# Layer 0 of a four-layer graph network: the bias of r and the candidate written into PSUM by ScalarE instead of two matmuls

## The chip, the core and the metric

One core of a Trainium2 chip runs the whole kernel in one launch. The metric is the device time of the launch in microseconds (us). A profile is taken of one further execution; its span goes from the first to the last instruction of the program, and the execution's own time is about 2 us longer.

## The reference, cut to what matters

Four layers follow each other, each with a residual and a layer norm. Layer 0 is a recurrence over the 256 nodes of each of 64 graphs, with 256 features. It is the only layer that the change touches:

```python
d = jnp.sum(adj, axis=-1)
dinv = jnp.where(d != 0, 1.0 / jnp.where(d != 0, d, 1.0), 0.0)
norm_adjT = jnp.swapaxes(adj, 1, 2) * dinv[:, :, None]

def step(h, i):
    x = jnp.take(h_e, i, axis=1)
    row = jnp.take(norm_adjT, i, axis=1)
    x_par = jnp.einsum('bj,bjd->bd', row, h)
    iou = x @ W_ioux.T + b_ioux + x_par @ W_iouh.T + b_iouh
    r, z = jnp.split(iou, 2, axis=1)
    r, z = (jax.nn.sigmoid(r), jax.nn.sigmoid(z))
    hc = jnp.tanh(x @ W_coux.T + b_coux + x_par * r @ W_couh.T + b_couh)
    h_new = z * x_par + (1.0 - z) * hc
    h = jax.lax.dynamic_update_slice(h, h_new[:, None, :], (0, i, 0))
    return (h, None)
```

Step i needs the state that step i - 1 has just written (through `x_par`), so the 256 steps can't run side by side. Layers 1 to 3 are a graph convolution, a masked attention and an eight-head attention, each done for one graph after another.

## The kernel before, in words

The layout of a state is 128 partitions by 128 columns: partition `o * 64 + b` holds graph b and the half o of the 256 features. The products need the features on partitions, so `xp` (the reference's `x_par`) and `rx` (r times `xp`) are transposed by TensorE and copied to SBUF by ScalarE (`flip`, L594 to L599, giving `xpT` and `rT`).

Layer 0 is one loop over the step n (L706 to L843). The order in which the instructions are written is the order on every engine's queue; no scheduler moves them. T = 32 steps share tables, U = 8 steps share a tile of sums `ACC`, and p = n % 8 decides which side work a step carries. Each step does this:

- The transpose of `xp` on TensorE, and its copy `xpT` on ScalarE. VectorE adds the state h of the step before (L630), ScalarE copies it to `hs` (L632).
- `h_part` multiplies `xpT` with the weights of r (four matmuls, L746) and of z (four, L768). Between and after them stand pieces of side work that TensorE does for later steps: `late` (p from 0 to 3) and `early` or the x side (p from 4 to 7).
- VectorE pushes h into the sums of the next steps (`push`, L614), GpSimd into those further away (`push_far`, L641 to L650), and GpSimd makes `ready` for the next step (L751 to L755).
- ScalarE takes the sigmoid of r (L776), the sigmoid of -z (`zc`, L780) and of z (L781). VectorE multiplies r with `xp` (`rx`, L778).
- `flip` transposes `rx` and copies it to `rT` (L782).
- For the next step, a new PSUM tile `rc` (two of them in turn, a bank each; it holds r in its first 128 columns, the candidate in its last) gets its bias (`bias_part`, L788) and the first half of its x products (L789).
- `h_part` adds the candidate's products with `rT` (L790).
- ScalarE copies up to two PSUM banks of side work to SBUF (`next_of(copies, n)`, L791 and L811). TensorE goes on with the second half of the x products (L798), and the bias and x products of the next z (L799 to L802).
- ScalarE takes the tanh of the candidate (L805). VectorE makes `v` from `ready` (L796), then `zcc` = (1 - z) times the candidate (L807), then the next `xp` (L810).

`bias_part` is one bf16 matmul for each half o, with a contraction of three: the bias is split into three bf16 parts, and the stationary operand is three rows of ones. It opens the accumulation in the bank; all the other products add:

```python
nc.tensor.matmul(
    G[o * B:(o + 1) * B], ones3, bias3[:, o, gates], start=True, stop=False,
    skip_group_check=True,
)
```

`G` is the PSUM tile, `gates` picks r and candidate (columns 0 and 1, so 256 columns) or z (column 2, so 128). PSUM is full: three banks for side work, two for `rc`, one each for z, for the transposes and for `keep`, which holds states and intermediates.

Of the kernel before, what the change touches and what calls it, by code (L numbers as in the profile page):

```python
# [9 lines left out]
F32 = mybir.dt.float32  # L10
# [9 lines left out]
P = 128  # L20
# [50 lines left out]
def _recurrence(tc, ident, Hd, x, adj, W_ioux, b_ioux, W_iouh, b_iouh, W_coux, b_coux, W_couh, b_couh):  # L71
# [18 lines left out]
    nc = tc.nc  # L90
# [12 lines left out]
    with ExitStack() as ctx:  # L103
        const = ctx.enter_context(tc.tile_pool(name="r_const", bufs=1))
# [2 lines left out]
        WhT = const.tile([P, 2, 2, 3, P], F32, name="WhT")  # L107
        bias3 = const.tile([3, 2, 3, P], BF16, name="bias3")
        ones3 = const.tile([3, B], BF16, name="ones3")
        tri = const.tile([P, P], F32, name="tri")  # L110
        window = [const.tile([P, T], F32, name=f"window{w}") for w in range(2)]
        dinv = const.tile([P, N], F32, name="dinv")
# [10 lines left out]
        with tc.tile_pool(name="r_setup", bufs=1) as tmp, tc.tile_pool(  # L123
            name="r_setup_ps", bufs=2, space=bass.MemoryType.PSUM
# [59 lines left out]
        with tc.tile_pool(name="r_first", bufs=2) as tmp, tc.tile_pool(  # L184
            name="r_first_ps", bufs=4, space=bass.MemoryType.PSUM
# [27 lines left out]
        ps = ctx.enter_context(tc.tile_pool(name="r_ps", bufs=1, space=bass.MemoryType.PSUM))  # L213
# [356 lines left out]
        def bias_part(G, gates):  # L570
            for o in range(2):
# [5 lines that stand above are left out]
        def x_part(G, n, kc, gates):  # L577
            a, u = divmod(n, U)
            h, i = divmod(u, U // 2)
            for o in range(2):  # L580
                nc.tensor.matmul(  # L581
                    G[o * B:(o + 1) * B], xqT[a, i // 2][:, i % 2, kc, h * B:(h + 1) * B],
                    WxT[:, kc, o, gates], start=False, stop=False, skip_group_check=True,
                )
# [9 lines left out]
        def flip(src, tag, n):  # L594
            pt = ps.tile([P, P], F32, tag="flip", name=f"{tag}_ps_{n}")
            nc.tensor.transpose(pt, src, ident)  # L596
            t = new(tag, n, 1)
            nc.scalar.copy(t, pt)  # L598
            return t  # L599

        def new(tag, n, bufs=2):
            return work.tile([P, P], F32, tag=tag, name=f"{tag}_{n}", bufs=bufs)
# [7 lines left out]
        def push(count):  # L610
            for _ in range(min(count, len(pushes))):
                m, j = pushes.pop(0)
                acc, s = cell(j, m)
                nc.vector.scalar_tensor_tensor(  # L614
                    acc[:, 0, :], keep[:, j % 2, :], s, acc[:, 0, :], ALU.mult, ALU.add
                )
# [56 lines left out]
        rc = ps.tile([P, 2, P], F32, tag="rc", name="rc_0", bufs=2)  # L673
        z = ps.tile([P, P], F32, tag="z", name="z_ps_0")
        for G, gates in ((rc, slice(0, 2)), (z, 2)):
            bias_part(G, gates)
            for kc in range(2):
                x_part(G, 0, kc, gates)

# [26 lines left out]
        for now in range(N):  # L706
            n = now
            k, i = divmod(n, T)
            p = n % U
            last = n + 1 == N  # L710
# [37 lines left out]
                push(1)  # L748
            if not last:
                kk, ii = divmod(n + 1, T)  # L750
                ready = new("ready", n)  # L751
                nc.gpsimd.tensor_mul(  # L752
                    ready, sums[(n + 1) // U][:, (n + 1) % U, :],
                    dinv[:, n + 1:n + 2].to_broadcast([P, P]),
                )  # L755
# [23 lines left out]
            zc = new("zc", n, 1)  # L779
            nc.scalar.activation(zc, z, AF.Sigmoid, scale=-1.0)  # L780
            nc.scalar.activation(z, z, AF.Sigmoid)  # L781
            rT = flip(rx, "rT", n)  # L782
            push(1)
            zx = keep[:, 2, :]
            nc.vector.tensor_mul(zx, z, xp)
            if not last:
                rc = ps.tile([P, 2, P], F32, tag="rc", name=f"rc_{n + 1}", bufs=2)
                bias_part(rc, slice(0, 2))  # L788
                x_part(rc, n + 1, 0, slice(0, 2))  # L789
            h_part(c, 1, rT)  # L790
            for _ in range(2 if p == 3 else 1):  # L791
# [513 lines left out]
@with_exitstack  # L1305
def kernel(ctx: ExitStack, tc: tile.TileContext, ins, out):
    nc = tc.nc
    x, adj = ins["x"], ins["adj"]
    B, N, D = x.shape
    main = ctx.enter_context(tc.tile_pool(name="main", bufs=1))  # L1310
    dram = ctx.enter_context(tc.tile_pool(name="dram", bufs=1, space=bass.MemoryType.DRAM))
    ident = main.tile([P, P], F32, name="ident")
    make_identity(nc, ident)
    Hd = dram.tile([N, B, D], F32, name="Hd")
    _recurrence(
        tc, ident, Hd, x, adj,
        *(ins["L0_gnn_" + n] for n in (
            "W_ioux", "b_ioux", "W_iouh", "b_iouh", "W_coux", "b_coux", "W_couh", "b_couh"
        )),
    )  # L1320
    l2, l3 = (
        {w + n: ins[f"{l}_gnn_{w}{n}"] for w in "Wb" for n in "vkqo"} for l in ("L2", "L3")
    )
    Yd = dram.tile([B, P, 2, D], F32, name="Yd")
    found = _layers(tc, ident, Hd, Yd, x, adj, ins["L1_gnn_W"], ins["L1_gnn_b"], l2, l3, out)
    with tc.If(found > 0):
        _layer_3(tc, ident, Yd, adj, l3, out)
# [36 lines left out]
```

## Time and profile before

| what | value |
|---|---|
| median of 3 runs | 3620.76 us (3611.67 to 3627.42) |
| profiled execution, its own time | 3625.61 us |
| its span | 3623.6 us |
| layer 0's steps in it | about 150 to 1590 us |
| granted TensorE clock | 0.975 |
| busy over the span | PE 92%, PEld 66%, DVE 66%, ACT 51%, POOL 41% |
| bias matmuls of rc (L572) | 512, median 292 ns |
| bias matmuls of z (L572) | 512, median 238 ns |

PE is TensorE's matmuls, PEld its weight loads, DVE VectorE, ACT ScalarE, POOL GpSimd, SP the queue that issues most DMAs. Matmuls are pipelined, so the length of one bar is longer than the time that it keeps the next one waiting; the starts of neighbours tell more. A row of the timeline has the start and the length in us, engine, line, operation, the tile written and the tiles read, the shapes, a count, and in brackets the idle time of the engine before it and what ended it. In the table of waits, a row names who waited, for whom, the total in us, the number of times and the longest. A row of the groups ends with the busy time in us, the mean length in ns, and the idle time before it.

### The profile page before, as it was taken

Reading aid. Unit: us, or ns where it says so; the run is one execution under the profiler, and the core shown is the slowest. Engines: PE = TensorE matmul, PEld = TensorE weight load, DVE = VectorE, ACT = ScalarE, POOL = GpSimd, SP = SyncE. Lnnn points to the kernel's source line nnn. Section 1 sums busy time; section 2 is a strip of 40 time slices with the busy share of each in tenths; the row PEclk is TensorE's granted clock in tenths of the full one; section 3 lists DMA queues with packets and bytes.
Section 4 is the critical chain, followed back from the end, with each engine's and each line's share of the span. In section 5 each row is a group of like instructions: output and inputs, shape, how many; then the busy total and the mean of one; then the engine's idle time right before and its main releaser. Section 6 shows DMA issues by size and latency. Waiting matters only on the chain.

```text
span 3623.6 us, 81902 instructions
## 1 busy us (share of the span) xinstructions
PE 3338.4 (92%) x30882; PEld 2384.0 (66%) x30882; DVE 2374.3 (66%) x7052; ACT 1836.0 (51%) x4771; POOL 1487.7 (41%) x1669
## 2 busy tenths in 40 slices
PE   5599999999989998858999999999999999999998
PEld 4455555555555555536777777777777777777776
DVE  2366766766667777734777677666677777776765
ACT  0144444444434444424666666666666666666664
POOL 2266666766556777722222222222222222222221
PEclk9799999999999999978999999999999999999999
DMA  8746566687876563240111111111111111111100
GB/s 279 219 129 142 155 170 154 147 189 201 192 186 167 150 165 106 67 107 29 45 45 45 45 45 45 45 45 45 45 45 45 45 45 44 43 45 45 45 27 22
DMA packets 389637, 348.51 MB, mean 96 GB/s; under 512 B 107244, under 2 KB 355192, under 8 KB 384120
## 3 DMA queue, kind: packets, MB, share of 16 engines
q1 hardware_dynamic: 367280, 323.84, 33.6%
q10 hardware_dynamic: 21960, 19.41, 1.6%
q8 instruction: 245, 4.01, 0.5%
q14 instruction: 152, 1.25, 0.1%
HBM read 224.01 MB, written 99.61 MB: 89 GB/s over the span
## 4 chain that ended last, share of the span: by engine, by line
PE 74%; POOL 6%; DMA 6%; DVE 6%; issue 4%; ACT 3%; SPq 2%; ACTq 0%; DVEq 0%; POOLq 0%
PE mm L940 13%; PE o L1143 7%; PE rc L581 4%; PE rc L589 4%; PE s L1123 4%; PE mm_2f L940 3%; PE mm_3v L940 3%; PE mm_3f L940 3%; PE mm_t L940 3%; PE mm_g L940 3%; PE mm_2s L940 3%; PE mm_2v L940 3%; PE mm_2w L940 3%; PE late L505 3%; PE tr_x L930 3%
## 5 line engine op out<-in xcount | busy, mean ns | idle before, releaser
L614 DVE SCALAR_TENSOR_TENSOR ACC<-keep,S,ACC 128x128 f32<-128x128 f32 x1712 | 504.5, 345 | 191.4 <-ACT hs L632 175.8
L909 POOL TENSOR_TENSOR rstd<-rstd,mhalf 128x2 f32<-128x2 f32 x256 | 173.1, 694 | 627.8 <-DVE rstd L908 626.1
L650 POOL TENSOR_TENSOR ACC<-ACC,far 128x384 f32<-128x384 f32 (+1 forms) x313 | 371.9, 1188 | 24.5
L1130 DVE TENSOR_TENSOR p<-s,neg 128x512 f32<-128x512 f32 x512 | 317.7, 683 | 68.6 <-PE s L1123 68.6
L581 PE MATMUL rc<-WxT,xqT 128*64 128x256 f32 x2048 | 329.8, 401 | 1.8 <-issue 1.8
L917 ACT ACTIVATE y<-y,shift,rstd 128x256 f32<-128x256 f32 x512 | 273.5, 598 | 95.3 <-DVE shift L915 91.0
L1035 POOL TENSOR_TENSOR y<-y,g 128x512 f32<-128x512 f32 x64 | 81.2, 1269 | 565.4 <-issue 556.4
L646 POOL TENSOR_TENSOR far<-hs,S 128x384 f32<-128x384 f32 (+1 forms) x313 | 304.8, 974 | 4.7
L1131 ACT ACTIVATE p<-p 128x512 f32<-128x512 f32 x512 | 295.0, 627 | 2.6 <-DVE p L1130 1.6
L752 POOL TENSOR_TENSOR ready<-ACC,dinv 128x128 f32<-128x128 f32 x255 | 102.3, 401 | 419.0 <-DVE ACC L614 397.9
L905 DVE BATCH_NORM_STATS2 st<-y 128x6 f32<-128x256 f32 x512 | 209.1, 408 | 93.8 <-POOL y L1035 89.0
L1158 DVE TENSOR_TENSOR y<-y,mm_3f 128x512 f32<-128x512 f32 x64 | 44.0, 688 | 281.3 <-PE mm_3f L940 281.3
L1149 DVE RECIPROCAL rT<-o 128x256 f32<-128x256 f32 x128 | 224.1, 1751 | 0.3 <-PE o L1143 0.3
L1046 ACT ACTIVATE qk<-mm,b_cols 128x256 f32<-128x256 f32 x256 | 107.4, 470 | 202.6 <-PE mm L940 202.6
L1021 ACT COPY xT<-tr_x 128x512 f32<-128x512 f32 x192 | 112.4, 587 | 182.7 <-PE tr_x L930 182.7
L589 PE MATMUL rc<-WhT,xpT 128*64 128x128 f32 x2048 | 170.2, 287 | 28.1 <-ACT xpT L598 28.0
L598 ACT COPY xpT<-xpT_ps 128x128 f32<-128x128 f32 x256 | 68.3, 267 | 245.5 <-PE xpT_ps L596 245.5
L589 PEld LDWEIGHTS rc<-WhT,xpT 128*64 128x64 f32 x2048 | 107.7, 137 | 117.8 <-ACT xpT L598 84.1
L807 DVE TENSOR_TENSOR zcc<-zc,rc 128x128 f32<-128x128 f32 x256 | 72.8, 284 | 155.1 <-ACT rc L805 155.1
L581 PE MATMUL z_ps<-WxT,xqT 128*64 128x128 f32 x2048 | 171.0, 289 | 0.0
L940 PE MATMUL mm<-xT,W2q 128*128 128x256 f32 x512 | 129.4, 396 | 44.7 <-ACT xT L1021 44.7
L1098 ACT ACTIVATE qk<-mm,b_cols 128x256 f32<-128x256 f32 x256 | 107.5, 471 | 118.2 <-PE mm L940 118.2
(165 smaller groups left out, 7980.2 us busy)
## 6 DMA issues: line engine op xcount, KB each, us to landing
xX<-in_x_dram ACTq DMA_DIRECT2D x16, 1024.0 KB
Us<-xu SPq DMA_DIRECT2D x64, 256.0 KB
rows<-in_adj_dram SPq DMA_DIRECT2D x64, 256.0 KB
ACC<-Us SPq DMA_DIRECT2D x32, 512.0 KB
xq<-in_x_dram SPq DMA_DIRECT2D x64, 256.0 KB
Hw<-hs SPq DMA_DIRECT2D x512, 32.0 KB
Es<-eu SPq DMA_DIRECT2D x64, 256.0 KB
early_sb<-Es SPq DMA_DIRECT2D x32, 512.0 KB
```

What stands on the lines that cost most here:

```text
L581: nc.tensor.matmul(G[o * B:(o + 1) * B], xqT[a, i // 2][:, i % 2, kc, h * B:(h + 1) * B], WxT[:, kc, o, gates], start=False, stop=False, s ...
L589: nc.tensor.matmul(G[o * B:(o + 1) * B], hT[:, kc * B:(kc + 1) * B], WhT[:, kc, o, g], start=False, stop=(kc == 1), skip_group_check=True,)
L614: nc.vector.scalar_tensor_tensor(acc[:, 0, :], keep[:, j % 2, :], s, acc[:, 0, :], ALU.mult, ALU.add)
L646: nc.gpsimd.tensor_mul(tmp[:, 0:count, :], hs.unsqueeze(1).to_broadcast(shape), s.unsqueeze(2).to_broadcast(shape),)
L650: nc.gpsimd.tensor_add(acc, acc, tmp[:, 0:count, :])
L905: nc.vector.bn_stats(st, y[:, c, :])
L917: nc.scalar.activation(y[:, c, :], y[:, c, :], AF.Identity, bias=shift[:, c:c + 1], scale=rstd[:, c:c + 1],)
L940: nc.tensor.matmul(pm[:, c, :], lhsT[:, k, c * P:(c + 1) * P], rhs[:, k, :], start=(k == 0), stop=(k == 1),)
L1130: nc.vector.tensor_add(p, s_ps[i], self.neg3)
L1131: nc.scalar.activation(p, p, AF.Exp, scale=ISQ)
L1143: nc.tensor.matmul(o_ps[i * HD:(i + 1) * HD, part, :], ones if part else self.v3_sb[:, k, h * HD:(h + 1) * HD], self.ps_of[hc][i][:, k, :] ...
L1149: nc.vector.reciprocal(rT, o_ps[:, 1, :])
```

## The change

A new SBUF tile `bias_rc` (128 x 256 fp32) keeps the bias of r and candidate as it stands in PSUM: it is copied once, from the first `rc`, right after `bias_part` has filled it. From step 1 on, the next `rc` gets its bias by a ScalarE copy of `bias_rc`, which stands on ScalarE's queue after the sigmoid of z and ahead of the copy `rT`. The x and h products then add to what ScalarE wrote; none of them opens the bank. In step 0 the next `rc` still gets its bias by matmuls, so both banks of `rc` have been opened once. The bias of z stays a matmul. To make room, `ready` has one buffer instead of two.

```diff
         ones3 = const.tile([3, B], BF16, name="ones3")
+        bias_rc = const.tile([P, 2, P], F32, name="bias_rc")
...
             bias_part(G, gates)
+            if G is rc:
+                nc.scalar.copy(bias_rc, rc)
             for kc in range(2):
...
-                ready = new("ready", n)
+                ready = new("ready", n, 1)
...
             nc.scalar.activation(z, z, AF.Sigmoid)
+            if not last:
+                rc = ps.tile([P, 2, P], F32, tag="rc", name=f"rc_{n + 1}", bufs=2)
+                if n:
+
+                    nc.scalar.copy(rc, bias_rc)
+                else:
+                    bias_part(rc, slice(0, 2))
             rT = flip(rx, "rT", n)
             push(1)
             zx = keep[:, 2, :]
             nc.vector.tensor_mul(zx, z, xp)
             if not last:
-                rc = ps.tile([P, 2, P], F32, tag="rc", name=f"rc_{n + 1}", bufs=2)
-                bias_part(rc, slice(0, 2))
                 x_part(rc, n + 1, 0, slice(0, 2))
             h_part(c, 1, rT)
```

In the program as built, the instructions of VectorE, GpSimd and SP keep their order. TensorE loses 508 bias matmuls and the loads of ones before them; its first x product of each step waits for ScalarE's copy. ScalarE gains 254 copies and the one into `bias_rc`. A separate instruction that waits for a semaphore of TensorE stood ahead of the `zc` sigmoid; it now stands ahead of the r sigmoid.

## The prediction

> **What bounds the kernel now.** I read the page first, then the chain of waits, then the table of waits over the 256 steps of layer 0 (150 to 1590 us of the span), then the timeline of single steps.
>
> ```profile
> PE 74%; POOL 6%; DMA 6%; DVE 6%; issue 4%; ACT 3%; SPq 2%; ACTq 0%; DVEq 0%; POOLq 0%
> ```
> The chain of the whole span lies mostly on PE. Inside layer 0 a step (1440 / 256 = 5.6 us) is a loop over all engines, and the table of waits of this stretch says who is late (total us, times, longest):
>
> ```profile
> DVE ACC L614 <- ACT hs L632: 175.8, 248, 1.8
> DVE zcc L807 <- ACT rc L805: 154.0, 162, 5.7
> ```
> In 162 of 256 steps VectorE stands idle before `zcc` until ScalarE's tanh is out: there, getting the candidate's products earlier makes the step shorter. In the other 94 VectorE is still busy with pushes when the tanh is ready, as here (timeline, step 147; the tanh is at 1004.86):
>
> ```profile
> 1004.17 1.25 DVE L614 SCALAR_TENSOR_TENSOR ACC<-keep,S,ACC 128x128 f32<-128x128 f32 x4
> 1005.34 0.28 DVE L807 TENSOR_TENSOR zcc<-zc,rc 128x128 f32<-128x128 f32 x1
> ```
> Now the stretch that the change touches (timeline, next step; first column start, second duration):
>
> ```profile
> 1008.09 0.28 ACT L780 ACTIVATE zc<-z_ps 128x128 f32<-128x128 f32 x1 [0.23 <-PE z_ps L589]
> ...
> 1008.26 0.27 ACT L781 ACTIVATE z_ps<-z_ps 128x128 f32<-128x128 f32 x1
> ...
> 1008.56 0.14 PEld L596 LDWEIGHTS rT_ps<-ident,rx 128*128 128x128 f32 x1 [0.49 <-DVE rx L778]
> ...
> 1008.82 0.10 PEld L572 LDWEIGHTS <-ones 3*64 3x64 bf16 x2
> ...
> 1008.98 0.27 ACT L598 COPY rT<-rT_ps 128x128 f32<-128x128 f32 x1 [0.45 <-PE rT_ps L596]
> 1009.04 0.20 PEld L581 LDWEIGHTS rc<-WxT,xqT 128*64 128x64 f32 x4
> ...
> 1009.31 0.58 PEld L589 LDWEIGHTS rc<-WhT,rT 128*64 128x64 f32 x8
> 1009.52 0.61 PE L589 MATMUL rc<-WhT,rT 128*64 128x128 f32 x8
> ```
> I count from the transpose of rx (1008.56 = 0): bias at 0.26, x products at 0.48, candidate's products at 0.96. The copy `rT`, which they need, ends at 0.69. So PE's own queue, not `rT`, holds them by some 0.2 us. These four offsets are nearly the same in nine tenths of the steps.
>
> **What the skill says.** "ScalarE: Activation LUTs", section What ACT_TABLE_LOAD costs: an instruction with immediate operands takes 186 ns + 0.833 ns an element, neighbours overlap by about 93 ns, a table load takes 1283 ns. The trace agrees: 627 ns for L1131 (512 elements, SBUF to SBUF: 186 + 427 = 613), zc to z start 0.17 after each other at 0.28 length, and the load is below. "PSUM — Partial Sum Buffer", section The four PSUM rules: ScalarE's writes leave the accumulation bits as they are, and a matmul that doesn't open adds where the bit is set. Step 0 still opens both rc banks, so the sums should stand; the trace of before has no such case. "Perfetto Trace Analysis", section Per-instruction lifecycle: a bar ends before its semaphore has spread. Here: `xpT` ends at 161.27, the weights that wait for it start at 161.31, so 0.05 us.
>
> **The change, part by part.**
> *Taken from PE:* two bias matmuls per step before the x products. Price: 1009.04 - 1008.82 = 0.22 us of PE per step, 254 steps.
> *Added to ScalarE:* one 128x256 copy, SBUF to PSUM, between the z sigmoid and the copy `rT`. No such row exists. Copies from PSUM give
>
> ```profile
> L231 ACT COPY lb<-late 128x512 f32<-128x512 f32 x240 | 139.0, 593 | 0.1
> L598 ACT COPY rT<-rT_ps 128x128 f32<-128x128 f32 x256 | 68.1, 266 | 147.0 <-PE rT_ps L596 146.3
> L917 ACT ACTIVATE y<-y,shift,rstd 128x256 f32<-128x256 f32 x512 | 273.5, 598 | 95.3 <-DVE shift L915 91.0
> ```
> Between 266 and 593 the line at 256 elements is 375 ns (low end); the page gives 186 + 213 = 399; L917, with two operand columns more, took 598 (high end). I take 0.40. A gain in place of a cost is excluded for the copy as such: it is new work.
> *On ScalarE's queue* `rT`, then the bank copies and the tanh stand behind it. In this step it starts 0.17 after z and frees the queue 0.30 later (0.40 less the overlap of 0.10), at about 1008.74; `rT` comes at 1008.98. ScalarE's idle time before `rT` is 146.3 us in 249 steps, 0.59 on average, against 0.30 needed: cost nothing. If that cover were gone, every 0.1 us would lie fully on the path.
> *A wait moves:* in the changed program as built, the separate semaphore instruction that stood before `zc` now stands before the r sigmoid. With it the sigmoid comes 0.11 after PE's end (`zc`: h products of z end 1007.98, start 1008.09), without it 0.05 (r: 1007.55, 1007.59). So z and the bias copy come 0.06 earlier, r comes 0.06 later. The latter is hidden where VectorE's pushes hold `rx` back; by the timeline `rx` starts right on r in 27 steps: 27 x 0.06 = 1.6 us lost.
> *PE's new wait:* the x products wait for the bias copy; behind them the candidate's products, the rest of x and z. In this step: z at -0.30, 0.06 earlier, +0.17, +0.40, +0.05: x products at 0.26, just when PE is free of the transpose. They last 0.48, to 0.74; `rT` is there at 0.69 + 0.05 = 0.74. Candidate at 0.74 plus some 0.05 of uncovered weight load, against 0.96: 0.17 gained. In the next step (z 0.22 before its transpose) x products come at -0.22 - 0.06 + 0.17 + 0.45 = 0.34: 0.14 gained. In about a quarter of the steps z is later, -0.15: 0.07. Mean 0.12.
> *PE's second wait* at this place is for its own old products, long done: nothing.
> *Total:* 162 x 0.12 = 19.4 us. In the other 94 steps VectorE is late: nothing. Of the 19.4, some is taken back by waits whose time is not PE's: the chain has POOL 6% and SP's queue 2% of 3623.6 (290 us, all taken as layer 0's) and landings of late_sb 2.7% of 1440 (39 us), 329 of 1440 or 23%. Left 15.0.
> *Once:* the table load of the sigmoid now stands behind the wait for r's products of step 0. Before, it ran ahead of it:
>
> ```profile
> 153.29 1.28 ACT L776 ACT_TABLE_LOAD   x1
> 156.47 0.26 ACT L776 ACTIVATE rc<-rc 128x128 f32<-128x128 f32 x1 [1.90 <-PE rc L589]
> ```
> Cost 1.3 us, in full. The one copy into bias_rc at 120 us lies in ScalarE's idle time before 124 us: nothing.
> *`ready` with one buffer:* GpSimd must wait for `v` of the step before. It waits anyway for pushes that VectorE does after `v` (397.9 us in 207 steps): nothing; at most its 0.40 us in a step where GpSimd is late.
> Sum: -15.0 + 1.6 + 1.3 = -12 us: the profiled execution from 3625.6 (span 3623.6 and 2 around it) to 3613.6. It lies 5 above the median of the three runs shown, 3620.8; taken from that: **3609 us**.
>
> **Rivals.**
> (a) *More of it stays.* If the copy takes 0.375 and the idle time of GpSimd and DMA absorbs nothing, all 162 steps gain up to 0.17: 27.5 - 3 = 24.5, so 3596; about 3598 as a case. For: in the last quarter of layer 0 the chain shows hardly any GpSimd. Against: z late in a quarter of the steps.
> (b) *The gain is absorbed.* Late landings (10 waits of GpSimd for late_sb, 35.6 us), GpSimd's far pushes and VectorE's own chain through `hs` set the pace, and the freed PE time becomes idle: 3620. For: VectorE's 248 waits on `hs`. Against: `hs` stands behind `xpT` on ScalarE, and this behind PE.
> (c) *Slower: PE waits for ScalarE.* The x products can't start before the bias copy. From 0.54 us of copy in a step with z at -0.22 (0.34 + 0.14 = 0.48, the old start) PE loses. At 0.60 and without z's 0.06 they start 0.12 late: 162 x 0.12 + 3 = 22 us, 3643; with z's 0.06, 13 us, 3634. For: L917's 598 ns. Against: that row has two operand columns, the copy none.
>
> **How the numbers follow.** Forecast 3603 to 3616 (its own range): 0.50. (a) 3590 to 3603: 0.25. (b) 3616 to 3625: 0.13. (c) above that: 0.12. The range leaves out (c) and the end of (a): 3594 to 3625. About 0.5% (18 us) is what a measurement of this kernel can tell from no change. Faster by more than that is under 3602.7: case (a) and a little of the forecast, 0.27; slower by more is over 3638.9: the worse part of (c), 0.06; the rest 0.67.
>
> **What would show it.** A row of 128x256 copies into rc, 254 of them, near 0.40 us; x products 0.26 to 0.41 after the transpose instead of 0.48, candidate's products at 0.78 to 0.90 instead of 0.96; the wait of `zcc` on the tanh smaller; `rT` still 0.42 after the transpose; the table load right before the first r sigmoid. A copy over 0.54 us, `rT` later than 0.42, or a wait of PE on ScalarE ahead of the x products that lasts past 0.48 would make the forecast wrong; so would steps of unchanged length in spite of earlier candidates.

## The result, and the profile after

| | before | after |
|---|---|---|
| device time, median of 20 runs each | 3620.95 us | 3610.8 us |
| lowest to highest | 3611.67 to 3628.59 | 3599.32 to 3617.62 |
| ratio, with its 95% interval | | 0.9967 (0.9956 to 0.9977) |
| span of the profiled execution | 3623.6 us | 3611.1 us |
| layer 0 in it, from rx's transpose of step 1 to that of step 255 | 1426.4 us | 1411.7 us |
| everything behind that | 2034.3 us | 2035.6 us |

The kernel became faster by 0.3%, 10 us between the medians and 12 between the means. In the two traces the whole difference lies in layer 0 (14.7 us, of which the start of the loop and the later layers give 2.2 back). The forecast was 3609.

First the new group of instructions, and the copy behind it on ScalarE's queue (groups of 150 to 1590 us; the last column is ScalarE's idle time ahead):

```profile
L789 ACT COPY rc<-bias_rc 128x256 f32<-128x256 f32 x254 | 92.2, 363 | 0.0
...
L599 ACT COPY rT<-rT_ps 128x128 f32<-128x128 f32 x256 | 67.9, 265 | 91.3 <-PE rT_ps L597 81.6
```

The copy takes 363 ns. Ahead of `rT` ScalarE now waits 81.6 us for TensorE where it waited 146.3: it used its spare time, and there was enough of it.

The same step 148 as in the prediction (timeline, TensorE and ScalarE lines of it):

```profile
994.37 0.36 ACT L789 COPY rc<-bias_rc 128x256 f32<-128x256 f32 x1
...
995.31 0.14 PEld L597 LDWEIGHTS rT_ps<-ident,rx 128*128 128x128 f32 x1 [1.27 <-DVE rx L781]
...
995.57 0.20 PEld L582 LDWEIGHTS rc<-WxT,xqT 128*64 128x64 f32 x4
...
995.73 0.27 ACT L599 COPY rT<-rT_ps 128x128 f32<-128x128 f32 x1 [1.00 <-PE rT_ps L597]
...
996.04 0.42 PEld L590 LDWEIGHTS rc<-WhT,rT 128*64 128x64 f32 x8 [0.28 <-ACT rT L599]
...
996.05 0.66 PE L590 MATMUL rc<-WhT,rT 128*64 128x128 f32 x8
```

From the transpose of rx (995.31): x products at 0.26 instead of 0.48, `rT` at 0.42 as before, the candidate's matmuls at 0.74 instead of 0.96. The tanh behind them comes only 0.18 earlier, at 1.44 instead of 1.62. Before, the candidate's weight loads began 0.21 ahead of their matmuls (1009.31 and 1009.52 in the prediction's lines), now 0.01: that is the uncovered load of 0.05 that the prediction counted. Here the bias copy was done long before. In the next step it wasn't:

```profile
1000.84 0.36 ACT L789 COPY rc<-bias_rc 128x256 f32<-128x256 f32 x1
1000.92 0.14 PEld L597 LDWEIGHTS rT_ps<-ident,rx 128*128 128x128 f32 x1 [0.41 <-DVE rx L781]
...
1001.25 0.20 PEld L582 LDWEIGHTS rc<-WxT,xqT 128*64 128x64 f32 x4 [0.19 <-ACT rc L789]
```

The x products start at 0.33, 0.05 us after the copy's bar ends at 1001.20. That is the new wait of TensorE on ScalarE. The table of waits (150 to 1590 us; total us, times, longest) has its size, beside those that the prediction showed and the side work's:

```profile
DVE ACC L615 <- ACT hs L633: 175.6, 248, 3.5
...
DVE zcc L815 <- ACT rc L813: 132.1, 131, 4.9
...
POOL ACC L827 <- DMA late_sb<-Lb: 41.1, 10, 8.5
...
PEld rc L582 <- ACT rc L789: 34.3, 167, 0.4
```

VectorE's wait for the tanh fell from 154.0 us in 162 steps to 132.1 in 131: less is left to gain there. The wait on `hs` has not moved. Step 147 (p = 3) shows why a part of the steps gains nothing. Its tanh is now out at 991.06 (it starts at 990.76 and lasts 0.30), but by its bars VectorE is in its pushes until 991.40, so `zcc` follows them and not the tanh:

```profile
990.15 1.25 DVE L615 SCALAR_TENSOR_TENSOR ACC<-keep,S,ACC 128x128 f32<-128x128 f32 x4
991.32 0.28 DVE L815 TENSOR_TENSOR zcc<-zc,rc 128x128 f32<-128x128 f32 x1
```

And the table load of step 0, which now stands behind the wait for r's products:

```profile
157.02 1.28 ACT L779 ACT_TABLE_LOAD   x1 [2.60 <-PE rc L590]
158.32 0.26 ACT L779 ACTIVATE rc<-rc 128x128 f32<-128x128 f32 x1
```

The chain over the whole span hardly shows a change of this size:

```profile
PE 71%; DVE 7%; DMA 7%; POOL 5%; issue 4%; ACT 4%; SPq 2%; ACTq 0%; DVEq 0%; POOLq 0%
```

So I measured steps. Worked out from the trace: the time from one transpose of rx to the next, medians for each p = n % 8, in us.

| p | 0 | 1 | 2 | 3 | 4 | 5 | 6 | 7 |
|---|---|---|---|---|---|---|---|---|
| before | 5.161 | 5.164 | 5.193 | 5.319 | 5.783 | 5.111 | 5.322 | 5.482 |
| after | 4.985 | 5.159 | 5.187 | 5.318 | 5.611 | 4.960 | 5.307 | 5.461 |
| `zcc` earlier by | 0.176 | 0 | 0 | 0 | 0.176 | 0.147 | 0.085 | 0.150 |
| each step against the same step of before | -0.176 | -0.006 | -0.006 | -0.002 | -0.174 | -0.147 | -0.086 | -0.150 |

At p = 1, 2, 3 VectorE's pushes hold `zcc`. At p = 0, 4, 5 what `zcc` gains, the step gains. At p = 6 and 7 the medians of the two kernels differ by only 0.015 and 0.021, and that misleads: over a third of these steps are held up by something else (23 of 61 before and 21 after are long by the measure below), and the median lies near the border of the two sorts. The last row (median of the differences, from step 8 on) compares every step with the same step of before: there p = 6 and 7 too pass on what `zcc` gains. So in an undisturbed block of eight the change brings 0.75 us, and in all 254 steps 23.6.

Layer 0 became only 14.7 us shorter. In 180 of the 254 steps the difference is that of the last row within 0.1 us. In the other 74 it swings by up to 4 us either way, and together they take about 8.5 us back. Where that goes is the question of the experiments. A single pair of traces gives its size only roughly: in the run below that adds nothing but an unused copy, 57 steps swing in the same way, by -2.6 us together.

A second sum from the same starts separates two things. A step is called long if it is over 0.5 us above the median of before at its p. Before has 35 long steps among the 247 from step 8 on, and they cost 77.5 us over the medians; the other 212 lie 3.8 us below the medians together. After: 35 long steps, 80.8 us; the others 21.3 below. So ordinary steps gained 17.5 us, and long ones took 3.3 back: 14.2 in all. The 3.3 are not much more than such a sum scatters: with the unused copy, long steps cost 75.7.

### The profile page after: what moved, and what is told of

Same layout as the page of the kernel before. It is cut to its first block, busy times and chain, and to the rows that moved or that the text cites. A ratio compares the mean times of both kernels' runs of the same rounds, so it can differ in the third digit from the quotient of the medians.

```text
span 3611.1 us, 81391 instructions
## 1 busy us (share of the span) xinstructions
PE 3296.8 (91%) x30374; PEld 2341.3 (65%) x30374; DVE 2375.3 (66%) x7052; ACT 1904.6 (53%) x5026; POOL 1485.1 (41%) x1669
## 4 chain that ended last, share of the span: by engine, by line
PE 71%; DVE 7%; DMA 7%; POOL 5%; issue 4%; ACT 4%; SPq 2%; ACTq 0%; DVEq 0%; POOLq 0%
PE mm L948 13%; PE o L1151 7%; PE rc L590 4%; PE s L1131 4%; PE rc L582 3%; PE mm_2f L948 3%; PE mm_3v L948 3%; PE mm_3f L948 3%; PE mm_g L948 3%; PE mm_t L948 3%; PE mm_2s L948 3%; PE mm_2v L948 3%; PE mm_2w L948 3%; DVE ACC L615 3%; PE tr_x L938 3%
## 5 line engine op out<-in xcount | busy, mean ns | idle before, releaser
L651 POOL TENSOR_TENSOR ACC<-ACC,far 128x384 f32<-128x384 f32 (+1 forms) x313 | 371.5, 1187 | 24.6
L1043 POOL TENSOR_TENSOR y<-y,g 128x512 f32<-128x512 f32 x64 | 80.8, 1262 | 567.7 <-issue 556.8
L1008 POOL TENSOR_TENSOR dis<-dis,mhalf 128x2 f32<-128x2 f32 x64 | 44.1, 689 | 292.0 <-DVE dis L1007 292.0
```

The costliest lines, as they stand in the source:

```text
L651: nc.gpsimd.tensor_add(acc, acc, tmp[:, 0:count, :])
```

## The experiments

The theory: the gain is what the candidate's products come earlier (x products at 0.26 to 0.40 instead of 0.48), passed on where VectorE waits for the tanh; the rest is taken back by the side work (GpSimd's adds, landings). Rivals: TensorE's new wait eats part of the gain, the ScalarE time of the copy costs something elsewhere, or the pace is set by `hs` and VectorE anyway. Ratios below are against runs of the kernel before on the same chip.

**No bias at all.** The x products open the bank; no copy, no bias matmul. The bias of r and candidate is left out from step 1 on.

```diff
-                if n:
-
-                    nc.scalar.copy(rc, bias_rc)
-                else:
-                    bias_part(rc, slice(0, 2))
...
-                x_part(rc, n + 1, 0, slice(0, 2))
+                x_part(rc, n + 1, 0, slice(0, 2), True)
```

> Leaves the bias of r and candidate out from step 1 on (no bias matmul, no copy; the first x product opens the bank), so the r gate and the candidate lack their bias. Theory (TensorE's queue held the candidate's products, and what still holds them is the end of ScalarE's copy): the x products start 0.26 us after the transpose of rx in every step, where they are at 0.31 to 0.37 in most steps with the copy; candidate's products at 0.74 everywhere. Against the changed kernel p = 5, 6, 7 gain 0.08, 0.10, 0.08 us a step, 0.26 x 32 = 8 us, less a quarter that late transfers and GpSimd take back = 6, and 1.6 (r's sigmoid without the separate semaphore instruction) and 1.3 (table load early again): about 3602, ratio to before 0.9948. Rival (the copy's wait is hidden, or the rest of the gain is absorbed by VectorE): same as the changed kernel, 3611, ratio 0.997.

Measured: 3601.76 us, ratio 0.995 (0.9935 to 0.9965). x products at 0.26 and the candidate's at 0.74 in all eight kinds of steps. A bias that costs nothing would thus bring 20 us between the medians, of which the change has 10. `zcc` was earlier by 0.176 at p = 0, 4, 5, 6, 7 and by nothing at p = 1, 2, 3.

**Two copies.** The bias copy is made twice, so that TensorE has to wait.

```diff
                     nc.scalar.copy(rc, bias_rc)
+                    nc.scalar.copy(rc, bias_rc)
```

> The copy of the bias is done twice in a row; the second waits for the first. Theory (TensorE waits for the copy's end): the x products start at about 0.31 + 0.06 + 0.36 = 0.72 us after the transpose instead of 0.31 (before: 0.48), the copy rT is pushed back by 0.15, the candidate's products come at 1.20 (before: 0.97). Only p = 0, where z is early, still gains 0.17. A block of 8 steps: -0.17 (p 0), +0.17 +0.17 +0.03 (p 1 to 3, where VectorE hides the first part), +0.18 +0.25 +0.26 +0.25 (p 4 to 7) = +1.14 us, x 32 = 36 us over before: about 3655, ratio 1.009. Rival (only the time taken off TensorE counts, the copy lies in ScalarE's idle time however long): 3611, ratio 0.997.

Measured: 3642.5 us, ratio 1.0056 (1.0042 to 1.0069), so slower than before. Step 148 of it (timeline; rx's transpose is at 1010.46):

```profile
1009.49 0.37 ACT L789 COPY rc<-bias_rc 128x256 f32<-128x256 f32 x1
1009.89 0.38 ACT L790 COPY rc<-bias_rc 128x256 f32<-128x256 f32 x1
...
1011.14 0.42 PEld L590 LDWEIGHTS rc<-WhT,rT 128*64 128x64 f32 x8 [0.23 <-ACT rT L599]
```

This step has time for both copies, but the median step doesn't: there the x products are at 0.72, `rT` at 0.60, the candidate's products at 1.20, as foretold. So rival (c) of the prediction is real, and only the size of the copy kept it off. The loss of an undisturbed step was foretold well: each step against the same step of before, the medians lose 1.19 us in a block of eight (foretold 1.14), some 38 us in 254 steps. But layer 0 became only 19 longer: 90 steps that differ by other amounts give 19 us back. Long steps took 74.8 us instead of 77.5, and the others lost 21.1. So what holds steps up swallows a part of a loss, as it swallows a part of a gain, and the expectation had left that out.

**Copy earlier.** The copy stands ahead of r's sigmoid, right behind `hs`, so it is always done when TensorE comes to the x products.

```diff
+            if not last:
+                rc_next = ps.tile([P, 2, P], F32, tag="rc", name=f"rc_{n + 1}", bufs=2)
+                if n:
+                    nc.scalar.copy(rc_next, bias_rc)
             nc.scalar.activation(r, r, AF.Sigmoid)
```

> The copy of the bias stands ahead of the r sigmoid on ScalarE's queue, right after the copy hs, instead of after the z sigmoid. Theory (the copy's end holds the x products in p = 1 to 3 and 5 to 7): they start at 0.26 us in every step, candidate's products at 0.74, about 6 us less than the changed kernel: 3604, ratio 0.9955; ScalarE is idle for some 0.6 us ahead of the r sigmoid, the copy takes 0.27 of it, so r isn't late. Rival (ScalarE has no room there: r comes later by 0.1 or more and rx with it): 254 x 0.1 = 25 us lost, 3635. Second rival (no wait left to shorten): 3611.

Measured: 3604.29 us, ratio 0.9957 (0.9942 to 0.9972). The step of before once more (rx's transpose at 987.96):

```profile
986.45 0.38 ACT L782 COPY rc<-bias_rc 128x256 f32<-128x256 f32 x1
986.75 0.26 ACT L783 ACTIVATE rc<-rc 128x128 f32<-128x128 f32 x1
...
988.22 0.20 PEld L582 LDWEIGHTS rc<-WxT,xqT 128*64 128x64 f32 x4
```

x products at 0.26 and candidate's products at 0.744 everywhere, as without a bias. Between the medians that is 6.5 us below the change as it is, and in the traces layer 0 is 7.3 shorter (1404.4 against 1411.7): about what the wait of TensorE on the copy costs. The intervals of the two ratios overlap, so the sign of this difference is likely and not certain.

**The copy alone, without the rest.** The kernel before, with a 128x256 copy on ScalarE at the new place that nobody reads, from weights in SBUF to a spare tile in SBUF (not to PSUM), and `ready` with one buffer.

```diff
+            if n and not last:
+                nc.scalar.copy(spare, WxT[:, 0, 0, 0:2, :])
             rT = flip(rx, "rT", n)
```

> The kernel before, bias matmuls and all, with one more 128x256 ScalarE copy (SBUF to an unused SBUF tile) per step at the place where the changed kernel has its copy, and ready with one buffer: ScalarE's part of the change alone. Theory (rT has some 0.3 us of cover on ScalarE): rT still starts 0.42 after the transpose, time as before, 3621, ratio 1.000 within 0.001. Rival (the work on ScalarE ahead of rT costs something that TensorE's relief outweighs): every 0.05 us of a later rT is up to 0.05 x 160 = 8 us: 3629 or more.

Measured: 3622.23 us, ratio 1.000 (0.999 to 1.001). In step 148 (rx's transpose at 1009.22) the copy is put into time in which ScalarE waited:

```profile
1009.17 0.39 ACT L784 COPY spare<-WxT 128x256 f32<-128x256 f32 x1
1009.22 0.33 PE L597 MATMUL rT_ps<-ident,rx 128*128 128x128 f32 x1
...
1009.64 0.27 ACT L599 COPY rT<-rT_ps 128x128 f32<-128x128 f32 x1
```

`rT` still starts at 0.42. ScalarE's time for the copy and the single buffer of `ready` cost nothing that can be measured.

**Without GpSimd's adds.** Far pushes, early adds and late adds are left out of both kernels, so the sums lack those parts. Does more of the gain stay?

```diff
-            if far:
-                push_far(n - 1, hs, far[0], len(far))
-            if behind:
-                push_far(*behind.pop(0))
-            if p in (3, 4):
...
-            if p in (5, 6) and n + 8 - p in sides:
...
-                nc.gpsimd.tensor_add(part, part, sides[n + 8 - p][:, half])
```

Of the kernel before:

> The kernel before without three kinds of GpSimd additions: the far pushes, the early parts and the late parts (so most of each node's sum is left out; TensorE, ScalarE, VectorE and the transfers do all their work). It is the base for the next kernel: with these gone, GpSimd and the landings of the late parts can't hold a step. Expected about 42 us a block of 8 steps in place of 44.6, so 3620 - 32 x 2.6 = 3540, between 3500 and 3560.

Of the changed kernel:

> The changed kernel with the same additions left out. Theory (a quarter to a third of the gain is taken back by waits for GpSimd and for landings): against the base without these additions the change brings what undisturbed steps show, 0.176 (p 0), 0.174 (p 4), 0.147 (p 5), 0.09 (p 6), 0.15 (p 7) = 0.73 us a block, x 32 = 23, less 1.3 = 22 us, at least 18. Rival (the missing part is lost inside steps p 6 and p 7, at the copy hs and at rx, and not to GpSimd and transfers): 12 us as with them.

Measured: 3594.8 us and 3579.66 us. The base was missed by far: taking away most of GpSimd's work made the kernel only 0.8% faster (ratio 0.9921, 0.9902 to 0.994). The pair differs by 15.1 us with a standard error of 3.1, between the theory's 22 and the rival's 12. With the adds gone, another stall stood in their place, the landings of the states in the ring `Hw` (waits, changed kernel without the adds):

```profile
PE late L506 <- DMA Hw<-hs: 18.4, 5, 7.1
```

In the changed kernel itself this row has 2.9 us, and in the kernel before

```profile
PE late L505 <- DMA Hw<-hs: 2.2, 1, 2.2
```

That led to the last four runs.

**Without the ring's transfers.** `into_ring` (L637 of before) no longer sends the states to `Hw`, which stays zero, so the late sums lack them. The edit was made in both kernels, and in both kernels without GpSimd's adds.

```diff
             n, hs = ring_in.pop(0)
-            for o in range(2):
-                nc.sync.dma_start(Hw[n % W::W, :, o * P:(o + 1) * P], hs[o * B:(o + 1) * B])
```

> The kernel before, without the transfers of every state into the ring (Hw<-hs); Hw stays zero, so the late sums and layer 0's result lack the states. All arithmetic stays. In the profile of before, TensorE waits for these landings for only about 2 us of layer 0, so by themselves they cost little: 3612 to 3620 us. If SP's queue or the traffic of the ring sets the pace in layer 0, it is faster by 20 us or more.

> The changed kernel with the same left out. Theory (GpSimd's adds and the landings of late_sb take back a good third of the gain, the ring's landings nothing as long as GpSimd is busy): 9 to 13 us below the kernel before without the ring, as in the pair with the ring. Rival (the ring's landings take it back): 18 to 23 us below.

> The kernel before, without GpSimd's far pushes, early and late adds, and without the transfers into the ring; the base for the next run. With the adds alone left out, TensorE still waited for landings at the late matmuls for some 25 us; without the ring most of that is gone: 3570 to 3580 us. If the waits were due to other transfers, 3590 to 3595.

> The changed kernel with the same left out. Theory (what the pair without the adds lost to landings was the ring's): the medians of the eight kinds of steps gain 0.73 us together in a block, times 32 blocks is 23, so 21 to 24 us below the run before it. Rival (another wait took it back, such as the landings of Es or the order of the steps itself): again about 15 us below.

| left out | before | changed | difference of the medians (standard error of the means) | ordinary steps | long steps |
|---|---|---|---|---|---|
| nothing | 3620.95 | 3610.8 | -10.1 (1.7) | -17.5 | +3.3 |
| GpSimd's adds | 3594.8 | 3579.66 | -15.1 (3.1) | -17.1 | +2.2 |
| ring | 3579.13 | 3565.67 | -13.5 (3.2) | -18.3 | -6.2 |
| both | 3542.46 | 3517.86 | -24.6 (2.1) | -22.2 | +0.9 |

The last two columns are from the one profiled pair each, in us, worked out as above. The first expectation was wrong: without the ring's transfers, for whose landings TensorE waits some 2 us in layer 0, the kernel is 44 us faster (3622.94 on the same chip to 3579.13). Not all of that is the transfers'. In the traces layer 0 falls from 1426.4 to 1402.4 us (its long steps from 77.5 to 56.8), but the part behind it also falls, from 2034.3 to 2021.0. No ring transfer runs there; layers 1 to 3 then work on a layer 0 that is zero, and the granted clock from 1600 to 3480 us reads 1.00 instead of 0.99. In all four runs without the ring that part is 2020 to 2022 us, so it drops out of the differences in the table. The third was wrong in the same direction, 3542 where 3570 to 3580 were foretold, some 12 us of it behind layer 0. The fourth agrees: without ring and adds the change brings 24.6 us, which is all that undisturbed steps gain. The second lies by a little above the upper end of the theory's 9 to 13, with an error that doesn't exclude either theory.

What is clear of the noise is the step from the first row to the last: with both gone the change brings 14.5 us more. Either edit alone keeps some 3 to 5 more by these medians. Whether the two causes add up or stand in for each other is not shown, since the 6 us by which 14.5 exceeds the two together have a standard error of 5.3. Nor can one traced pair decide it: without the ring layer 0 became 25.0 us shorter in the traces, where the medians give 13.5.

Where does a transfer cost time that nobody is seen to wait for? First SP's own queue, kernel before (waits of the queue, 150 to 1590 us). L485 sends the late sums' parts, L639 the states to the ring, one behind the other in the same queue:

```profile
SPq L485 <- ACT lb L231: 158.9, 16, 24.0
SPq L639 <- ACT hs L632: 126.5, 51, 6.9
```

What stands behind such a wait leaves late. The wait alone proves no cost: without the ring's transfers the row of L485 has 253.6 us. GpSimd's wait for the landings of the late sums was 35.6 us in 10 waits before, as the prediction says; without the ring's transfers it is

```profile
POOL ACC L817 <- DMA late_sb<-Lb: 16.1, 5, 6.6
```

Next `hs` on ScalarE. The view of one line lists also the separate semaphore instructions of its queue (count: shortest/median/longest ns). Kernel before:

```profile
L632 ACTq EVENT_SEMAPHORE  x461: 17/38/2357, 200.1 to 1587.7; - x154
```

Without the ring:

```profile
L632 ACTq EVENT_SEMAPHORE  x249: 17/17/17, 198.3 to 1565.9; - x125
```

That looks like waits of up to 2.36 us for the buffers of `hs`, seven in turn, which the ring's transfers read. It is not. By the starts and ends in the trace of before, each of the 44 waits of over 0.15 us ends 0.04 us after VectorE has finished the state h (L630), and the table of waits has the longer ones in h's row:

```profile
ACT hs L632 <- DVE keep L630: 6.2, 8, 2.2
```

Without the ring this row still has 5.4 us in 9 waits; only the separate instruction for it is gone. So the ring's cost does not pass through `hs`. GpSimd's shorter wait for the late sums is the one route seen here, and that it carries the whole cost is not shown.

**A version that is better than both.** The early copy, and the bias of z written by ScalarE as well, right behind the copy `rT`; `zcc` has one buffer, for the room.

```diff
             h_part(c, 1, rT)
+            if not last:
+                z = ps.tile([P, P], F32, tag="z", name=f"z_ps_{n + 1}")
+                nc.scalar.copy(z, bias_z)
...
-                z = ps.tile([P, P], F32, tag="z", name=f"z_ps_{n + 1}")
-                bias_part(z, 2)
```

> The early copy (ahead of the r sigmoid) and also the bias of z by a 128x128 ScalarE copy, right after the copy rT. TensorE loses its last bias matmuls, 0.17 us a step between the second x part and the x products of z. Theory (the transpose of the next xp stands behind this queue by about 0.06 us in p = 0, 5, 6, 7, and by all of it in p = 4, where four more transposes stand there): 4 x 0.06 + 0.17 = 0.41 us a block, x 32 = 13, less a quarter = 10 under the early copy alone: 3594, ratio to before 0.993. Rival (from xp on VectorE's chain holds the step; or the copy of z pushes the bank copies and the tanh back): no better than the early copy alone, 3604, ratio 0.9955, or worse.

Measured: 3594.65 us, ratio 0.992 (0.9903 to 0.9938). Against the early copy alone the median of p = 4 fell from 5.607 to 5.237 and that of p = 5 from 4.935 to 4.832. Each step against the same step of the early copy, p = 0, 5, 6 and 7 gained 0.10 where 0.06 was foretold, and p = 4 gained 0.37 where 0.17 was. Not all of that is the bias of z: a separate semaphore instruction ahead of `rT` is gone in this run, `rT` starts at 0.367 instead of 0.422, and `zcc` comes 0.05 earlier at p = 0, 4, 5, 6 and 7. In layer 0 these gains would sum up to 25 us, and 9.0 arrived, so that the 10 foretold came out is luck. Ordinary steps are 36.5 us below before's, and long ones cost 6.3 more.

And with one sigmoid of a single column ahead of the loop, so that the table is loaded early:

```diff
+        nc.scalar.activation(keep[:, 0, 0:1], dinv[:, 0:1], AF.Sigmoid)
         xp = new("xp", 0)
```

> As the early copy with z, and one sigmoid of 128x1 elements ahead of the loop, so that the table load runs before step 0 needs it. Theory: the first r sigmoid starts 0.05 to 0.11 us after its products instead of 1.3 us later; 1.3 us less, once, which the profile shows and the median hardly does: 3593. Rival (the load was hidden by something else): no change in the time from the first transpose of xp to the first r sigmoid.

Measured: 3589.82 us, ratio 0.9907 (0.989 to 0.9924), faster than before and than the change, and the fastest of those that leave nothing out. Its load lies in a stretch in which ScalarE had to wait for TensorE anyway:

```profile
152.69 1.28 ACT L687 ACT_TABLE_LOAD   x1
153.98 0.17 ACT L687 ACTIVATE keep<-dinv 128x1 f32<-128x1 f32 x1
155.02 0.27 ACT L600 COPY xpT<-xpT_ps 128x128 f32<-128x128 f32 x1 [0.86 <-PE xpT_ps L598]
157.25 0.26 ACT L787 ACTIVATE rc<-rc 128x128 f32<-128x128 f32 x1 [1.97 <-PE rc L591]
```

r's sigmoid now starts 0.10 us after the end of its products (157.15), as foretold, where in the run before it 1.39 us lie between them. From the first transpose of `xp` to r's sigmoid it is 2.60 us, against 4.50, but that isn't the load alone: r's products took 1.12 us in the run before it and 0.66 here, at a granted clock of 0.55 and 0.81 (150 to 162 us). The 4.8 us between the two medians are more than this stretch explains, and the runs of the one spread over 13 us, so the size of this last step is not settled.

## Why the prediction was right, step by step

The time foretold, 3609, and the time measured, 3610.8, agree, and the mechanism is the one described. But two terms of the sum were off, in opposite directions, so that the agreement is this close is in part luck.

*TensorE freed by two bias matmuls (0.22 us).* Right. Without anything in their place the x products start at 0.26, as foretold.

*The copy takes 0.40.* Over-sized: 0.363, near the line through the two plain copies (0.375). The estimate by the Trainium skill ("ScalarE: Activation LUTs", What ACT_TABLE_LOAD costs: 186 ns and 0.833 an element), 399, was higher than the measurement, which decides; the 1283 ns of the same section for a table load are those of the traces. With that term 0.04 smaller, the x products came at 0.26 (p = 0, 4), 0.31 (p = 1, 2, 3), 0.34 (p = 5, 7) and 0.34 or 0.40 (p = 6, about half each), not at 0.26, 0.34 and 0.41. The 0.54 from which TensorE would lose was never near. Its reason held, though: with two copies the kernel was slower than before.

*A gain of 0.12 in 162 steps, 19.4 us.* The number of steps was right: `zcc` moves at five of eight p, 160 of 256. The size was too small: it moved by 0.176, 0.176, 0.147, 0.085 and 0.150, on average 0.147, so 160 x 0.147 = 23.5 us. The mis-sized term is the copy's.

*23% taken back, 4.4 us, and 1.6 for r's later sigmoid.* Too small. Of the 23.5, layer 0 kept 14.7 in the traces, so more than a third was taken back; between the means of 20 runs the change brought 12.1, about half. The prediction's own 19.4 - 4.4 - 1.6 is 13.4. So the sum came out by two errors that cancel. The shares of GpSimd and of SP's queue in the chain were a fair sign that something would be taken back, but no measure of how much. Which of it is whose: GpSimd's adds or the ring alone don't decide it; with both gone the change brings 24.6. That part is shown. Through which buffer or queue the disturbed steps lost it is not.

*z and bias copy 0.06 earlier, r 0.06 later.* Both seen: in the medians, z at -0.30 instead of -0.24, and at p = 1 r's sigmoid at 4.31 instead of 4.25 after the transpose of the step before. VectorE's wait of `rx` for r rose from 13.5 us in 13 steps to 17.3 in 18. The 1.6 us can't be told from the rest.

*`rT` not later, at no cost.* Right: 0.42 before and after, and the copy alone changed nothing (ratio 1.000).

*Table load, 1.3 us.* Right at its place: r's sigmoid starts 1.38 us after the end of its products (156.94 to 158.32), before 0.05 (156.42 to 156.47). From the first transpose of `xp` to r's sigmoid the step became only 0.7 us longer (3.84 to 4.53), but there TensorE was slower in before's profile, at a granted clock of 0.78 instead of 0.86 (150 to 162 us):

```profile
155.33 1.09 PE L589 MATMUL rc<-WhT,xpT 128*64 128x128 f32 x8
156.28 0.66 PE L590 MATMUL rc<-WhT,xpT 128*64 128x128 f32 x8
```

The first line is before's, the second that of the change.

*`ready` with one buffer, nothing.* Right as far as the run with the copy alone shows, which had it too.

*The rivals.* (a), more stays, would be the change with the early copy, 3604: a wait of TensorE on ScalarE stood between, not only the side work. Its "GpSimd and DMA absorb nothing" needs the ring and the adds gone. (b), all is absorbed, holds in the steps p = 1, 2, 3, where VectorE's pushes are late (which the forecast had left out already), and in some of the disturbed steps elsewhere. (c) is what two copies showed; one of 0.363 is short enough.

## What to carry to other kernels

Before work is moved from a full engine to one with spare time, find the instruction behind which it will stand and the latest time at which the full engine needs its result. Here moving the copy from behind three sigmoids to ahead of them gave some 6 us more between the medians (likely, not certain), beside the change's 10. In a loop over several engines, count in how many of the steps the wait is the last one, and then check whether an earlier start is really passed on to the next step. Compare each step with the same step of the other kernel: where half of the steps of a kind are held up, the medians of the two kernels can show no gain although every undisturbed step has it. And the table of waits is no price list: it gave the ring's landings 2 us, and without the transfers layer 0 was 24 us shorter.

## What the runs showed of the hardware that I had not expected

- A ScalarE copy of 128x256 fp32 from SBUF to PSUM took 363 ns as the bias copy, 376 as a second one right after it and 393 at the earlier place; from SBUF to SBUF it took 390.
- A separate semaphore instruction ahead of a ScalarE instruction is seen as some 0.055 us: in the runs where `rT` waits for TensorE without one (two copies), it starts at 0.367 after the transpose in the steps in which nothing else holds it, in the runs with one at 0.422.
- A table load isn't always done in idle time ahead of a wait: in the changed kernel it started only when the wait for TensorE was over (157.02, r's sigmoid at 158.32), and before the change it ran 3.2 us ahead of the sigmoid (153.29 to 156.47).
